# The output products of the last batch are begun inside the last attention units

## The chip, the cores and the metric

The kernel runs on one core of one Trainium2 chip, as a single launch. Times are device microseconds (us) of that core. The core's engines are named as in the profile: PE (TensorE, with PEld for its weight loads), DVE (VectorE), ACT (ScalarE), POOL (GpSimd) and SP (SyncE, which here only issues DMAs). "Line 913" or "L913" is a line of the kernel's file as the profile numbers it.

## The reference, cut to what matters

One block of a transformer with adaptive layer norm: attention, and then a mixture of eight experts in which every expert picks its 512 best rows. `x` is 8 batches of 1024 rows of 256; there are 16 heads of 64.

```python
mod = (_silu(c) @ wmod).reshape(8, 6, 1, -1)
sa, ca, ga, sb, cb, gb = (mod[:, i] for i in range(6))
# ga and gb are then kept at least 0.25 away from zero
h = _layernorm(x) * (1 + ca) + sa
x = x + ga * attention(h, w_qkv, w_o)
h = _layernorm(x) * (1 + cb) + sb
x = x + gb * experts(h, router_w, router_b, w1, b1, w2, b2)

def attention(inputs, w_qkv, w_o):
    q, k, v = three products of inputs with w_qkv, per head
    attn = softmax(einsum('bhqn,bhkn->bhqk', q, k) / 8)
    out = einsum('bhqk,bhkn->bhqn', attn, v)
    return concat_of_heads(out) @ w_o

def experts(x, ...):
    scores = softmax(x @ router_w + router_b)
    G, idx = top_k(scores.T, 512)      # over all 8192 rows
    y = scatter_add(relu(x[idx] @ w1 + b1) @ w2 + b2, times G)
```

The experts choose among all rows, so their search cannot begin before the router's scores of the last rows are known.

## The kernel before, in words

Attention is cut into 128 *units*. A unit is one batch, one pair of heads and one half (512) of the query rows; `unit(u)` gives them, two units to a pair, 16 to a batch. The last batch is number 7, and its pairs 4 to 7 are the last eight units; units 124 and 125 are pair 6, units 126 and 127 are pair 7. A unit has eight chunks of 128 keys. Per chunk, PE makes the scores (L397), ACT copies them out of PSUM (L406), DVE keeps the maximum (L414); when the maximum over all keys is turned and spread (L424 to L461), DVE subtracts it (L464), ACT takes the exponential (L467), PE multiplies with the values (L477), and POOL adds the exponentials of the chunks up for the denominator (L497, L500).

The order of all instructions is written by hand under a manual schedule: a loop over *steps*, four to a unit, so unit `u` begins at step `4u`. Its values are made six steps later (`LAG`). Everything that is not the core of a unit is put in by `at(step, place, function, ...)`; a step runs its places in a fixed order: "load" (DMA issues), "turn", the turned maximum, "head", scores, subtractions and maxima, "m1" (PE work ahead of the values), "post" (small DVE and ACT work), exponentials, values, sums on POOL, "pool", "m2". Each engine runs its own list in that order. G below stands for step 512, that of unit 127's turned maximum; the loop ends six steps later.

Denominators: `den_out` multiplies POOL's sum with ones (L516), ACT copies the result, and it goes to DRAM; `den_load` fetches it as 128 short rows, `den_inv` inverts it on DVE (L545) and stores it, `den_spread` reads it back spread over the partitions, `den_mul` scales the pair's rows on POOL (L562). Each of those DMAs is on SP's queue, in order. For pair 7 of batch 7, `last_load_den`, `last_inv` and `last_mul` do the same for each half, the second half on ACT's queue.

The output product `w_o` of a batch is made while the next batch's units run (`out_proj`, L618). The last batch has no next one. There the pairs 0 to 3 are loaded back in one DMA (`last_load`, step G-6, into the buffer of the large part of the projection weights, "wq1"), `last_gates` scales `wo` by the batch's gate on DVE (L738), and behind the loop a written list follows: for each tile of 128 rows, `add_pairs` makes eight pair products (L913), `add_x` adds the rows, takes mean and variance on DVE and the root of the variance on POOL (L106, L108) and starts the norm (L929), `norm` ends it (L937); then, for two tiles at a time, `turn` transposes them (L664), `route` makes the router's product (L676), and `score` takes the softmax (L691 to L707) and stores the rows. The sums of unit 127's chunks 0 to 3 come from POOL; chunks 4 to 7 of that unit are summed by PE (`pd_last`). After that the transposed scores (L1055) start the experts' search on DVE (L1068).

PSUM tiles come from pools: `ps_s` ("s") has two buffers, `ps_m` ("mm"), `ps_av` ("av") and `ps_b` ("less") one each; whoever takes a buffer waits until its former content has been read.

## Time and profile before

| what | us |
|---|---|
| median of 3 runs | 3381.17 |
| lowest and highest run | 3381.15, 3382.17 |
| the profiled execution | 3379.61 |
| its span, first to last instruction | 3377.9 |
| busy in the span: PE, DVE, ACT, POOL | 3312.0, 2718.1, 2468.7, 2716.6 |
| unit 127's maximum is turned | at 3013.39 |
| first output product of the last batch | at 3037.85 |
| the search starts on DVE | at 3076.09 |

Times with "at" count from the span's start. A line of the profile's timeline gives start, duration, engine, line, operation, what is written and read (with shapes) and how many instructions were merged; in brackets stands how long the engine was idle before it and what released it. In the groups of instructions, the columns behind the shape are the count, the busy time, the mean duration in ns, and the idle time before.

### The profile page before, as it was taken

Reading aid. Unit: us, or ns where it says so; the run is one execution under the profiler, and the core shown is the slowest. Engines: PE = TensorE matmul, PEld = TensorE weight load, DVE = VectorE, ACT = ScalarE, POOL = GpSimd, SP = SyncE. Lnnn points to the kernel's source line nnn. Section 1 sums busy time; section 2 is a strip of 40 time slices with the busy share of each in tenths; the row PEclk is TensorE's granted clock in tenths of the full one; section 3 lists DMA queues with packets and bytes.
Section 4 is the critical chain, followed back from the end, with each engine's and each line's share of the span. In section 5 each row is a group of like instructions: output and inputs, shape, how many; then the busy total and the mean of one; then the engine's idle time right before and its main releaser. Section 6 shows DMA issues by size and latency. Waiting matters only on the chain. (4 is left out here: it accounts for less than half of the span.)

```text
span 3377.9 us, 60194 instructions
## 1 busy us (share of the span) xinstructions
PE 3312.0 (98%) x23699; PEld 1343.1 (40%) x23699; DVE 2718.1 (80%) x3391; ACT 2468.7 (73%) x3079; POOL 2716.6 (80%) x1630
## 2 busy tenths in 40 slices
PE   9999999999999999999999999999999999986998
PEld 3333333333333333333333333333333333334666
DVE  6898888888888888888888888888888888886332
ACT  5888887778787877878787777878777787760221
POOL 4898888989898888989898888988898888891333
PEclk9999999999999999999999999999999999997999
DMA  4010012111121112111221112111221112124442
GB/s 83 17 46 28 26 48 56 42 47 53 45 63 42 47 53 56 44 47 51 47 61 42 47 53 56 48 42 52 48 59 42 47 53 58 51 77 145 108 100 45
DMA packets 184112, 183.68 MB, mean 54 GB/s; under 512 B 49148, under 2 KB 161292, under 8 KB 183700
## 3 DMA queue, kind: packets, MB, share of 16 engines
q1 hardware_dynamic: 167860, 158.44, 17.0%
q0 software_dynamic: 7168, 12.72, 1.9%
q10 hardware_dynamic: 8800, 8.68, 0.8%
q8 instruction: 186, 3.05, 0.4%
q14 instruction: 98, 0.80, 0.1%
HBM read 126.01 MB, written 62.16 MB: 56 GB/s over the span
## 5 line engine op out<-in xcount | busy, mean ns | idle before, releaser
L500 POOL TENSOR_TENSOR acc<-acc,p 128x1024 f32<-128x1024 f32 x764 | 1816.4, 2378 | 85.2 <-ACT p L467 37.4
L406 ACT COPY p<-s 128x1024 f32<-128x1024 f32 x1024 | 990.6, 1016 | 317.0 <-PE s L397 294.2
L464 DVE TENSOR_TENSOR p<-p,less 128x1024 f32<-128x1024 f32 x1024 | 1210.5, 1213 | 7.8 <-PE less L461 3.2
L414 DVE TENSOR_TENSOR top<-top,s 128x1024 f32<-128x1024 f32 x768 | 933.5, 1215 | 119.4 <-ACT p L406 104.5
L467 ACT ACTIVATE p<-p 128x1024 f32<-128x1024 f32 x1024 | 1025.3, 1052 | 3.4 <-DVE p L464 2.3
L397 PE MATMUL s<-qk,qk 64*128 64x512 f32 (+1 forms) x6144 | 996.6, 601 | 4.1 <-DVE top L414 4.1
L477 PE MATMUL av<-p,v 128*64 128x512 f32 x4096 | 995.1, 596 | 2.0 <-ACT p L467 2.0
L356 PE MATMUL pq<-hT,wq 128*64 128x512 f32 x2048 | 497.7, 607 | 0.7 <-ACT hT L308 0.7
L397 PEld LDWEIGHTS s<-qk,qk 64*128 64x128 f32 (+1 forms) x6144 | 314.8, 151 | 418.6 <-issue 218.5
L477 PEld LDWEIGHTS av<-p,v 128*64 128x64 f32 x4096 | 270.5, 137 | 487.1 <-issue 379.7
L497 POOL TENSOR_TENSOR acc<-p,p 128x1024 f32<-128x1024 f32 x128 | 304.8, 2381 | 15.9 <-ACT p L467 15.9
L432 DVE TENSOR_REDUCE tt<-tt 128x8 f32<-128x1024 f32 x128 | 157.7, 1232 | 178.6 <-PE tt L424 178.6
L356 PEld LDWEIGHTS pq<-hT,wq 128*64 128x64 f32 x2048 | 125.0, 136 | 350.3 <-issue 199.1
L377 PE MATMUL pv<-wq,hT 128*64 128x256 f32 x2048 | 249.2, 385 | 0.0
L634 POOL TENSOR_TENSOR ox<-ox,at 128x256 f32<-128x256 f32 x56 | 40.6, 726 | 243.2 <-DVE at L629 243.2
L618 PE MATMUL po<-wo,ot 128*64 128x256 f32 x1792 | 202.9, 379 | 0.0
L377 PEld LDWEIGHTS pv<-wq,hT 128*64 128x64 f32 x2048 | 135.7, 136 | 155.8 <-issue 57.1
L414 DVE TENSOR_TENSOR top<-p,s 128x1024 f32<-128x1024 f32 x128 | 154.8, 1209 | 46.9 <-ACT p L406 44.1
L618 PEld LDWEIGHTS po<-wo,ot 128*64 128x64 f32 x1792 | 128.7, 137 | 88.6 <-issue 24.3
L562 POOL TENSOR_TENSOR oT<-oT,rb 128x1024 f32<-128x1024 f32 x63 | 150.1, 2382 | 0.0
L1308 POOL DMA_INDIRECT out_dram<-eo,tok x32 | 53.6, 1675 | 115.8 <-DMA out_dram<-eo,tok 63.7
L361 ACT ACTIVATE qk<-pq 128x512 f32<-128x512 f32 x128 | 76.6, 598 | 95.7 <-PE pq L356 95.7
(198 smaller groups left out, 2254.2 us busy)
## 6 DMA issues: line engine op xcount, KB each, us to landing
rb<-rden_d SPq DMA_DIRECT2D x126, 256.0 KB
oT_d<-oT SPq DMA_DIRECT2D x60, 512.0 KB
ot<-oT_d SPq DMA_DIRECT2D x56, 512.0 KB
rows_d<-gb_d SPq DMA_DIRECT2D x8, 1024.0 KB
w<-in_L_ffn_w_dram SPq DMA_DIRECT2D x8, 1024.0 KB
w<-in_L_ffn_w_dram ACTq DMA_DIRECT2D x8, 1024.0 KB
rows_d<-row SPq DMA_DIRECT2D x62, 132.0 KB
lnx<-in_L_attn_inputs_dram SPq DMA_DIRECT2D x28, 256.0 KB
```

The source lines that it names most:

```text
L356: nc.tensor.matmul(pq[m * N : (m + 1) * N, :], wq_of(k, a, 2 * p + m), hTs[b][:, k, sl], start=(k == 0), stop=(k == KC - 1),)
L377: nc.tensor.matmul(pv[m * N : (m + 1) * N, i, :], hTs[b][:, k, t0 : t0 + N], wq_of(k, 2, 4 * g, 4), start=(k == 0), stop=(k == KC - 1),)
L397: nc.tensor.matmul(ps[k : k + n, j, :], kt[r, c * P + k : c * P + k + n], qt[r, h * QB : (h + 1) * QB], start=True, stop=True,)
L406: nc.scalar.copy(probs[u, c], ps)
L414: nc.vector.tensor_tensor(tops[u], probs[u, 0] if c == 1 else tops[u], ps, ALU.max)
L432: nc.vector.tensor_reduce(nm[:, 0, :], tt.rearrange("p r q k -> p q r k"), AX.XY, ALU.max, negate=True)
L464: nc.vector.tensor_tensor(probs[u, c], probs[u, c], less[u], ALU.add)
L467: nc.scalar.activation(probs[u, c], probs[u, c], AF.Exp)
L477: nc.tensor.matmul(avs[u][j * N : (j + 1) * N, :], v[:, c, hh * N : (hh + 1) * N], pT[:, j, :], start=(c == 0), stop=(c == NT - 1),)
L497: nc.gpsimd.tensor_tensor(sums[u], pts[0], pts[1], ALU.add)
L500: nc.gpsimd.tensor_tensor(sums[u], sums[u], pt, ALU.add)
L618: nc.tensor.matmul(po[m * N : (m + 1) * N, :], ot[:, p, m * N : (m + 1) * N], wo[:, p, :], start=(p == 0), stop=(p == NP - 1),)
```

## The change

It touches the last batch only.

- `part_out` makes the products of pairs 0 to 3 for the row tiles 4 to 7 at steps G-5, G-3, G-2 and G-1, and ACT copies each into a buffer; `part_add` adds all four to the rows of `x` on POOL. They need gated weights and the reloaded pairs early: `tail_set` (step G-56) takes the "wq0" buffer, loads the gate and builds a picking matrix, `tail_gate` multiplies four pairs of `wo` on POOL, and `tail_load` (formerly `last_load`) moves from step G-6 to G-9. `tail_gates` scales the other four pairs on DVE at step G.
- `fill` makes the pair products of tiles 0 and 1 between the units' work from step G to G+4, and all others behind the loop. Eight tiles share two PSUM tiles of `ps_s`.
- Pair 6 is handled in halves (`half_load`, `half_inv`, `half_spread`, `half_mul`), and the denominator of unit 125 moves from step G to G-1.
- Pair 7: `late_den` sums the chunks 4 to 7 on PE for unit 126 too; `late_inv` inverts the 128x256 denominators where they lie in PSUM, `late_spread` spreads them with two products by the picking matrix, `late_mul` scales. Nothing of it goes through DRAM.
- In `add_x` the first of the two variance steps is on DVE; the written list is reordered, and the norm of a tile (`add_norm`) stands behind the next tile's addition.

```diff
-            pool, tag = (ps_s, "s") if u == NSU - 1 else (ps_av, "av")
-            avs[u] = pool.tile([P, QB], F32, tag=tag, name=f"av{u}")
+            avs[u] = ps_av.tile([P, QB], F32, tag="av", name=f"av{u}")
...
+    def half_load(h):
+        d = tail["dq", h] = small.tile([P, 2 * QB // P], F32, tag="dq", name=f"dq_half{h}", bufs=2)
+        nc.sync.dma_start(
+            d, den_d[B - 1, NP - 2, h].rearrange("j s -> (j s)").rearrange("(p c) -> p c", p=P)
+        )
+
+    def half_inv(h):
+        nc.vector.reciprocal(tail["dq", h], tail["dq", h])
...
+    def half_mul(h):
+        at_hand[B - 1, NP - 2] = oTs[B - 1, NP - 2]
+        half = oTs[B - 1, NP - 2][:, h * QB : (h + 1) * QB]
+        nc.gpsimd.tensor_tensor(half, half, tail["rb", h], ALU.mult)
...
+        nc.sync.dma_start(tail["gate"], mod_d[B - 1 : B, :D].to_broadcast([P, D]))
+        nc.gpsimd.memset(tail["pick"], 0.0)
+        for j in range(2):
+            for i in range(2):
+                r = (2 * j + i) * 32
+                nc.gpsimd.memset(tail["pick"][r : r + 1, i, j * N : (j + 1) * N], 1.0)
+
+    def tail_gate(p):
+        nc.gpsimd.tensor_mul(tail["wo"][:, p, :], wo[:, p, :], tail["gate"])
+
+    def tail_gates():
+        w = wo[:, 4:, :]
+        nc.vector.tensor_tensor(
+            w, w, tail["gate"].unsqueeze(1).to_broadcast([P, NP - 4, D]), ALU.mult
+        )
...
+    def part_out(t):
+
+        if "part" not in tail:
+            tail["part"] = work.tile([P, 4, D], F32, tag="ot", name="part")
+        po = ps_m.tile([P, D], F32, tag="mm", name=f"part{t}")
+        add_pairs(po, t, 0, 4, 0, 3)
+        nc.scalar.copy(tail["part"][:, t - 4, :], po)
+
+    def part_add():
+        x1 = tail["x"][:, 4:, :]
+        nc.gpsimd.tensor_add(x1, x1, tail["part"])
...
+    def fill(t, p0, p1):
+        if not pos:
+            for i in range(2):
+                po = ps_s.tile([P, 2, QB], F32, tag="s", name=f"po_last{i}")
+                for k in range(4):
+                    pos[k // 2 * 4 + 2 * i + k % 2] = po[:, k % 2, k // 2 * D : (k // 2 + 1) * D]
+        add_pairs(pos[t], t, p0, p1, 0 if t < 4 else 4, NP - 1)
...
+    def late_inv(u):
+        tail["den"] = small.tile([P, QH], F32, tag="den", name=f"den{u}", bufs=2)
+        nc.vector.reciprocal(tail["den"], tail["pd"])
+
+    def late_spread(u):
+        rb = tail["rb"] = ps_m.tile([P, QB], F32, tag="mm", name=f"rb{u}")
+        for i in range(2):
+            nc.tensor.matmul(
+                rb[:, i * QH : (i + 1) * QH], tail["pick"][:, i, :], tail["den"],
+                start=True, stop=True,
+            )
...
-    for u in range(NSU - 1):
-        at(4 * u + 13 - max(0, u - NSU + 4), "m2", den_out, u)
+    for u in range(NSU - 2):
+        at(4 * u + (13 if u < NSU - 3 else 11), "m2", den_out, u)
...
-    at(4 * NSU - 2, "load", last_mods)
-    at(4 * NSU - 6, "load", last_load)
-    at(4 * NSU + 4, "load", last_load_den, 0)
-    at(4 * NSU + 4, "pool", last_gates)
-    at(4 * NSU + 5, "post", last_inv, 0)
+    G = 4 * NSU
+    at(G - 56, "load", tail_set)
+    for p in range(4):
+        at(G - 51 + 4 * p, "pool", tail_gate, p)
+    at(G - 9, "load", tail_load)
+    at(G - 2, "load", last_mods)
+    for t, g in zip((4, 5, 6, 7), (-5, -3, -2, -1)):
+        at(G + g, "m1", part_out, t)
+    for h, g in ((0, -2), (1, 0)):
+        at(G + g, "load", half_load, h)
+        at(G + g + 1, "post", half_inv, h)
+        at(G + g + 2, "load", half_spread, h)
+        at(G + g + 3, "pool", half_mul, h)
+    at(G, "post", tail_gates)
+    at(G, "m1", fill, 0, 0, 4)
+    at(G + 1, "m1", fill, 0, 4, 6)
+    at(G + 1, "m2", late_den, NSU - 2, range(4, NT))
+    at(G + 2, "post", late_inv, NSU - 2)
+    at(G + 2, "m1", fill, 0, 6, 7)
+    at(G + 2, "m1", fill, 1, 0, 4)
+    at(G + 3, "m1", late_spread, NSU - 2)
+    at(G + 3, "post", late_mul, NSU - 2)
+    at(G + 3, "m1", fill, 1, 4, 7)
+    for t in range(2):
+        at(G + 4, "m1", fill, t, 7, 8)
+        at(G + 4, "pool", add_x, t)
+    at(G + 4, "pool", part_add)
+    at(G + 5, "m1", late_den, NSU - 1, range(4, 6), False)
+    at(G + 5, "pool", add_norm, 0)
...
-                if u1 < NSU - 1 or gm1 < 2:
+                if u1 < NSU - 2 or gm1 < 2:
...
+        late_den(NSU - 1, range(6, NT), True, False)
...
-            (add_x, 0), (add_pairs, 3, 0, NP), (add_x, 1), (norm, 0), (add_x, 2), (norm, 1),
-            (last_mul, 1), (norm, 2), (add_x, 3), (add_pairs, 4, 0, NP), (norm, 3), (turn, 0),
-            (add_x, 4), (norm, 4), (add_pairs, 5, 0, NP), (add_x, 5), (route, 0), (norm, 5),
-            (turn, 2), (add_pairs, 6, 0, NP), (score, 0), (add_x, 6), (route, 2), (norm, 6),
-            (turn, 4), (add_pairs, 7, 0, NP), (score, 2), (add_x, 7), (route, 4), (norm, 7),
-            (score, 4), (turn, 6), (route, 6), (score, 6),
+            (late_inv, u), (fill, 2, 0, NP), (add_norm, 1), (late_spread, u), (late_mul, u),
+            (fill, 3, 0, NP), (add_x, 2), (turn, 0), (fill, 4, 4, NP), (add_x, 3), (add_norm, 2),
+            (route, 0), (fill, 5, 4, NP), (add_x, 4), (add_norm, 3), (turn, 2), (fill, 6, 4, NP),
+            (score, 0), (add_x, 5), (add_norm, 4), (route, 2), (fill, 7, 4, NP), (add_x, 6),
+            (add_norm, 5), (score, 2), (turn, 4), (add_x, 7), (add_norm, 6), (route, 4),
+            (add_norm, 7), (score, 4), (turn, 6), (route, 6), (score, 6),
```

## The prediction

> **What bounds the kernel now.** The page shows 98% busy for PE and 80% for DVE and POOL, but that is a mean over 3,378 us, and the change touches the last 90 us of attention only. So I read first the windows by stage (columns: stretch, its length, then busy us and instruction count of PE, PEld, DVE, ACT, POOL, the granted clock, DMA share, GB/s).

> ```profile
> 2987.00:3013.00 26.00, 21.77 (x152) 6.47 (x148) 24.34 (x30) 20.77 (x24) 22.93 (x18) 1.00 0.35 116
> 3013.00:3038.00 25.00, 17.70 (x148) 5.53 (x150) 17.12 (x22) 12.77 (x19) 24.45 (x11) 1.00 0.09 24
> 3038.00:3069.00 31.00, 31.00 (x316) 20.98 (x314) 16.24 (x49) 3.10 (x8) 10.14 (x22) 1.00 0.22 69
> 3069.00:3076.00 7.00, 2.70 (x30) 1.59 (x28) 3.75 (x16) 1.57 (x5) 5.20 (x23) 0.85 0.59 196
> ```

> The last two units have PE free for 4.2 and 7.3 us; then PE alone is the bound for 31 us; then a chain of small steps leads to the search. Next the timeline of PE in the third and fourth stretch (start, duration, what, idle before):

> ```profile
> 3037.28 0.64 PE L516 MATMUL pd_last<-acc,ones 128*32 128x256 f32 x8 [1.82 <-POOL acc L500]
> 3037.85 1.95 PE L913 MATMUL po_last<-wo,oT_last 128*64 128x256 f32 x16
> ...
> 3060.46 1.95 PE L913 MATMUL po_last<-wo,oT_last 128*64 128x256 f32 x16
> 3062.24 1.90 PE L913 MATMUL po_last<-wo,oT 128*64 128x256 f32 x16
> 3063.96 0.59 PE L676 MATMUL pl<-rw,h2T 128*64 128x8 f32 x16
> ...
> 3071.66 0.44 PE L664 MATMUL pth<-ident,rows_last 128*128 128x128 f32 x2 [2.13 <-DVE rows_last L937]
> ```

> The output products of all eight row tiles start only at 3037.85, when POOL's sum of unit 127 is in. One tile (eight pairs) takes 3063.96 - 3060.46 = 3.50, a pair 0.44. Then DVE's timeline, for the price of a tile and for the end of the stage:

> ```profile
> 3051.51 0.41 DVE L921 TENSOR_TENSOR x_last<-x_last,po_last 128x256 f32<-128x256 f32 x1
> 3051.96 0.43 DVE L116 BATCH_NORM_STATS2 st_b<-x_last 128x6 f32<-128x256 f32 x1
> 3052.42 0.18 DVE L117 BATCH_NORM_AGGREGATE mv_b<-st_b 128x2 f32<-128x6 f32 x1
> 3052.64 0.48 DVE L929 SCALAR_TENSOR_TENSOR row<-x_last,mv_b,mod 128x256 f32<-128x256 f32 x1
> 3053.04 0.48 DVE L937 SCALAR_TENSOR_TENSOR row<-row,rs_b,mod 128x256 f32<-128x256 f32 x1
> ...
> 3071.12 0.48 DVE L937 SCALAR_TENSOR_TENSOR rows_last<-rows_last,rs_b,mod 128x256 f32<-128x256 f32 x1 [0.43 <-POOL rs_b L108]
> ...
> 3076.09 0.75 DVE L1068 TENSOR_SCALAR half<-p_sc 128x256 int32<-128x256 int32 x2 [0.84 <-PE p_sc L1055]
> ```

> From start to start: the four steps before the norm take 0.45 + 0.46 + 0.22 + 0.40 = 1.53, the norm 0.40. The norm of tile 7 starts at N = 3071.12; the search starts 4.97 later. All behind that is moved as a whole, so the question is what N becomes. Last the groups by shape, for the reciprocals and the scaling of the weights:

> ```profile
> L545 DVE RECIPROCAL dq<-dq 128x16 f32<-128x16 f32 x63 | 14.6, 231 | 0.0
> L699 DVE RECIPROCAL rd<-rd 128x2 f32<-128x2 f32 x32 | 5.3, 166 | 1.1
> L738 DVE TENSOR_TENSOR wo<-wo,mod 128x1024 f32<-128x1024 f32 x2 | 5.0, 2534 | 0.0
> L629 DVE TENSOR_TENSOR at<-po,mod 128x256 f32<-128x256 f32 x56 | 23.7, 424 | 56.3 <-PE po L618 56.3
> ```

> **The change part by part.** Times are those of the profiled execution: 3379.61, of which the span is 3377.9; the median shown is 3381.17, 1.56 above it. G is the step of unit 127's transposed maximum, 3013.39 before.

> *Tiles 4 to 7, pairs 0 to 3, at steps G-5, G-3, G-2, G-1.* Four groups of 4 pairs, 1.75 each, 7.0 of PE. From 2987.42 (scores of step G-5) PE's list up to the maximum of unit 127 is: ten score chunks 9.35, ten value chunks 9.0, the four groups 7.0, two denominators 1.14, transposes 0.72 + 0.45, row spread 0.65: 28.3, so the maximum is turned at 3015.7 instead of 3013.39. PE had 4.2 idle there, so 7.0 costs 2.3. DVE, some 0.75 late after the first group, is ready at 3014.1 and no longer the bound. Four ACT copies of 0.38 lie beside DVE.

> *Denominator of unit 125 from step G to G-1.* 0.57 on PE (in the sum above). At 3019.59 the routing product sat 1.42 behind that denominator's copy; this goes.

> *Pair 6 in halves.* SP: store, load, store, two spreads per half. Half 0's load stands behind the load of `mod7`, issued 3009.14 when POOL finished the last row of batch 6; its inverse (0.2) comes on DVE after the last maximum at 3014, 2 us after landing. Half 1: copied 3015.8, loaded by about 3020 to 3022 (the rows for such a load, 3038.39 to 3043.60, give 5.2), inverted on DVE at 24.9 between two subtractions, 2.7 to 4.8 spare. It would hold DVE's subtractions, so exponentials, values and all behind, if late. Cost: 0.4 of DVE.

> *Loads moved.* `tail_load` (2048 + 1024 KB) goes from 2981.46 to about 2960, when the last weights are read (PE 2957.99 + 1.94). In the windows that transfer filled 2983 to 2992, about 9 us. Behind it in SP's queue now are an output store (2966.39), `ox` and `ot` (2967.58), which PE wants at 2983.87; at worst they are done near 2976. Cost nothing, 8 us of cover. `tail_set` at G-56 and its five fills and four products on POOL, 0.73 each, some 4 us in all: POOL stood idle 4.22, 0.64 and 2.17 before three late L634, which takes them up.

> *Weights scaled once, at step G:* 2.53 on DVE, in a hole of 4.00 behind the split maximum (DVE waited for the routing product until 3020.28). Ready at 3021.1; subtractions start at 3021.5, before 3020.59. Before it was 4.99 at 3030, also hidden.

> *Unit 126's chunks 4 to 7 summed by PE instead of POOL:* 4 x 0.45 = 1.8 more on PE, 9.7 less on POOL, whose last sum then ends by 3032 and ends the wait of 1.82 at 3037.28.

> *Last denominators on chip.* Twice a reciprocal 128x256. No row has that; 128x2 takes 166 ns and 128x16 231, so 4.6 ns an element and 1.35 for 256. Ends: 0.42 (L629, as many elements, one pass) and 1.75 (from the dearest 128x16 row, 253 ns); I take 1.35, the slope of most rows. [...] Two picking products of 128x256 each time: 0.22 per record, two records each, 0.88; ends 0.44 and 1.75. In exchange two round trips through DRAM go, the second 3038.39 to 3053.44; PE never waited for it, so that alone is worth nothing.

> *PE from the maximum at 3015.7 to the last denominator:* turn 0.7, 16 pair products 7.0, 12 value chunks 10.8, row turns and spread 0.5, routing 0.57, ten denominator groups 4.5, picks 0.88: 25.0. The pick waits for the reciprocal: subtractions from 3021.5, six at 1.145 plus 0.2, plus 1.35 gives 3029.95, where PE arrives at 3029.7: 0.3 more. End 3041.0, against 3037.85 before, but with 32 of 64 pair products done.

> *From there.* PE: tile 2 3.5, pick 0.88, tile 3 3.5: 3048.9 (call it E). By the order of the built program the addition of tile 2 waits for tile 3's product, that of 4 for 5's, and 6 for 7's, since tiles share a PSUM tile. A tile on DVE now is 1.53 plus 0.20 for the variance step moved from POOL (ends 0.16 and 0.25), 1.72. DVE after E: two tiles 3.44, norm 0.40, router 0.40; waits for tile 5's product until E+4.77; tile 4 and norm 3 to E+6.89; now the score of tiles 0, 1 wants an exponential that ACT has queued behind the copy of tiles 2, 3's transposes, which wait for norm 3: transposes 0.48, copy 0.68, exponential 0.5, and DVE stands until E+8.5; scores 0.62, tile 5 1.72, norm and router 0.80, tile 6 1.72, norm and scores 1.02, tile 7 1.72, norm 0.40, router 0.40: N = E+16.95 = 3065.85. PE needs only E+11.4 for all its products: DVE is the bound. Gain 5.25.

> *What is late next.* POOL fills its constants after the score copies of tiles 4, 5, which now stand ahead of them: the last constant is in at N+6.5 where the search wants it at N+6.1: 0.45 lost. Weights and rows land far ahead of the first expert product (3127.79).

> Sum: -5.25 + 0.45 = -4.8: 3374.8 on the profiled execution's scale, **3376.4** on the median's.

> Unknown: reciprocals -0.4 to +0.4, picks -0.9 to +1.7, variance step 0.3 either way, hops between engines 0.8, PE's clock when the experts start (first relus 0.85 apart, later half that, so about 1 either way). Together -7.0 to -2.3.

> **The rivals.**
> - *PE stays the bound to the end*: additions start with their own tile and the exponential does not hold DVE. Then tile 7's product ends at E+9.3, N = E+11.7 and the gain is 10.5 less 0.45: 3371.1. For it: before, DVE hardly made PE wait in this stretch. Against: DVE's list from E to N is 14.8 long without any hole, so it needs both; the hole alone gone gives N = E+15.2, a gain of 6.5, 3374.7.
> - *Nothing comes of it*: the four groups cost their whole 7.0 (score chunks arrive late and DVE's maxima too), 4.7 more than in the sum: 3381. For it: DVE was 94% busy there. Against: its maxima had the scores early.
> - *Slower: half 1's denominators land late and hold DVE's queue.* Its load is behind a spread that waits for POOL's product of pair 5 (3013.77) and a buffer. Beyond 2.7 to 4.8 late, every us is one us; 11.6 more makes it slower by 0.2%, 3388. For it: the similar load before held DVE for 8.46. Against: SP's queue is otherwise empty here.

> **How the numbers follow.** Two runs of this kernel can be told apart at about 0.2%, 6.8 us. My sum (-7 to -2.3, nearly all within 0.2%) 0.55; PE-bound end 0.23, most of it faster by over 0.2%; nothing 0.10; slower, by the queue, 0.12. With the sum's own edge: faster 0.25, same 0.63, slower 0.12. The likeliest case's own range is 3374.2 to 3379.0. For 8 in 10 I take 3371.5 (the PE-bound end) to 3380.5.

> **What would show it.** Unit 127's maximum turned near 3015.7, its last denominator on PE near 3041, no POOL wait before it; a DVE wait of about 2 us on ACT's exponential at the first score; N near 3065.9; reciprocal 128x256 about 1.35. Wrong if DVE waits for `dq_half1`, if PE has holds between 3016 and 3041, or if DVE's tiles take other than 1.7.

## The result, and the profile after

The changed kernel takes **3376.17 us** (median of 20 runs, 3375.05 to 3378.03), the kernel before 3381.16 beside it (20 runs, 3380.21 to 3383.82): a ratio of 0.9985, 95% interval 0.9978 to 0.9992. The interval lies below 1, so the kernel is faster, but by less than the 0.2% (6.8 us) from which the prediction counts a change; the time is 0.2 us from the forecast. A repeat of both, later, gave 3376.79 against 3379.82, 0.9990 (0.9981 to 0.9999), so the gain is 3 to 5 us, and the hit to 0.2 is partly luck.

The profiled execution after has 3377.24, its span 3375.4, against 3379.61 and 3377.9. Single executions differ by 1 us ahead of the part that was changed. So all places below are counted from **S**, the start of the scores of step G-5, the last thing on PE ahead of the first part group: 2987.42 before, 2988.35 after. First the windows by stage of the kernel after (columns as before):

```profile
2987.00:3013.00 26.00, 26.00 (x202) 10.66 (x200) 23.78 (x30) 19.54 (x24) 22.96 (x18) 1.00 0.18 52
3013.00:3038.00 25.00, 25.00 (x234) 12.07 (x234) 19.40 (x31) 14.78 (x20) 16.85 (x9) 1.00 0.10 29
3038.00:3069.00 31.00, 25.89 (x240) 14.83 (x230) 17.88 (x59) 3.71 (x10) 8.41 (x15) 0.93 0.17 57
3069.00:3076.00 7.00, 2.85 (x36) 1.96 (x36) 3.66 (x15) 1.08 (x3) 5.67 (x28) 0.50 0.63 194
```

PE, which had 4.2 and 7.3 us free in the first two stretches, has none now; in the third, which it filled before, it has 5.1 free. The granted clock in the third fell from 1.00 to 0.93. PE's timeline of the kernel after shows where:

```profile
3016.37 0.67 PE L424 MATMUL tt<-ident,top 64*128 64x64 f32 x16
...
3041.72 1.95 PE L630 MATMUL po_last<-tail_set,tail_rest 128*64 128x256 f32 x16
...
3049.99 0.66 PE L779 MATMUL pth<-ident,row 128*128 128x128 f32 x4
...
3056.90 0.44 PE L779 MATMUL pth<-ident,row 128*128 128x128 f32 x2 [1.81 <-DVE row L705]
3057.27 3.34 PE L630 MATMUL po_last<-wo,oT 128*64 128x256 f32 x16
3060.38 0.91 PE L791 MATMUL pl<-rw,h2T 128*64 128x8 f32 x16
3061.14 1.93 PE L630 MATMUL po_last<-wo,oT 128*64 128x256 f32 x16
```

The turned maximum comes at S+28.0, the first product behind the last denominator at S+53.4 (call it T0), the end of tile 3's product, E, at S+61.6. Then PE stands 1.81 for DVE's norm of tile 3, and tile 6's half product (its pairs 4 to 7) takes 3.1 from start to start instead of 1.75. On DVE's timeline of the kernel after, the additions (L687) and the end:

```profile
3050.11 0.42 DVE L687 TENSOR_TENSOR x_last<-x_last,po_last 128x256 f32<-128x256 f32 x1 [2.86 <-PE po_last L630]
...
3054.76 0.42 DVE L687 TENSOR_TENSOR x_last<-x_last,po_last 128x256 f32<-128x256 f32 x1 [0.70 <-PE po_last L630]
...
3058.43 0.17 DVE L813 TENSOR_REDUCE rd<-ex 128x2 f32<-128x16 f32 x1 [1.59 <-ACT ex L806]
...
3063.12 0.42 DVE L687 TENSOR_TENSOR x_last<-x_last,po_last 128x256 f32<-128x256 f32 x1 [1.40 <-PE po_last L630]
...
3067.88 0.48 DVE L705 SCALAR_TENSOR_TENSOR tail_set<-tail_set,rs_b,mod 128x256 f32<-128x256 f32 x1
...
3073.35 0.76 DVE L1131 TENSOR_SCALAR half<-p_sc 128x256 int32<-128x256 int32 x2 [0.84 <-PE p_sc L1118]
...
3074.94 0.17 DVE L1145 TENSOR_SCALAR cand<-upto 128x4 f32<-128x4 f32 x1 [0.33 <-POOL upto L1114]
```

Additions 2, 4 and 6 each wait for PE's next tile, and the first score waits 1.59 for an exponential. N, the norm of tile 7, is at S+79.53 (before S+83.70), the search at S+85.00 (before S+88.67): 3.7 earlier. From the search to the end the profile has 302.05 after and 301.8 before. Last the group of the new reciprocal:

```profile
L667 DVE RECIPROCAL den<-pd 128x256 f32<-128x256 f32 x2 | 3.5, 1754 | 2.4 <-PE pd L515 2.4
```

### The profile page after: what moved, and what is told of

It is laid out like the page before. It is cut to its first block, busy times and chain, and to the rows that moved or that the text cites. A ratio compares the mean times of both kernels' runs of the same rounds, so it can differ in the third digit from the quotient of the medians.

```text
span 3375.4 us, 60263 instructions
## 1 busy us (share of the span) xinstructions
PE 3317.2 (98%) x23739; PEld 1346.8 (40%) x23739; DVE 2718.8 (81%) x3399; ACT 2470.6 (73%) x3081; POOL 2711.8 (80%) x1629
```

## The experiments

The theory at the start: PE's free time in the last two units now holds 14 us of products, which is the gain, and from E on DVE bounds the end; the rivals were PE as the bound to the end, and early products that are worth nothing. In what follows, the part groups are the products of `part_out`, a pick is the pair of products by the picking matrix (L672), a turn is PE's transposing of two tiles (L779), and the hole is DVE's wait of 1.59 at the first score. Each run was timed against the kernel before on the same chip. All that was measured, with places from S:

| kernel | T0 | E | N | search | median | before beside it | ratio, 95% interval |
|---|---|---|---|---|---|---|---|
| before | 50.43 | | 83.70 | 88.67 | 3381.16 | | |
| after | 53.37 | 61.64 | 79.53 | 85.00 | 3376.17 | 3381.16 | 0.9985 (0.9978 to 0.9992) |
| after, repeated (r1) | 53.37 | 61.64 | 79.52 | 84.99 | 3376.79 | 3379.82 | 0.9990 (0.9981 to 0.9999) |
| no part groups (e1) | 51.38 | 59.65 | 82.77 | 88.26 | 3380.39 | 3380.47 | 1.0001 (0.9991 to 1.0010) |
| tiles 0, 1 late (e2) | 50.63 | 65.80 | 82.03 | 87.50 | 3379.90 | 3380.47 | 1.0000 (0.9991 to 1.0009) |
| the same, pick later (e2b) | 49.06 | 64.24 | 80.58 | 86.06 | 3378.16 | 3381.28 | 0.9991 (0.9982 to 1.0000) |
| neither early start (e7) | 47.05 | 62.23 | 85.36 | 90.83 | 3383.96 | 3380.83 | 1.0008 (0.9999 to 1.0017) |
| before + PE's sums (b1) | 49.65 | | 82.94 | 88.48 | 3380.74 | 3381.28 | 0.9998 (0.9989 to 1.0007) |
| denominators by DRAM (e6) | 53.39 | 60.44 | 79.39 | 85.15 | 3376.07 | 3379.82 | 0.9989 (0.9980 to 0.9998) |
| exponential early (e3) | 53.38 | 61.65 | 79.51 | 84.98 | 3376.04 | 3380.47 | 0.9987 (0.9978 to 0.9996) |
| PE kept busy (e4) | 53.38 | 61.65 | 77.87 | 83.35 | 3375.24 | 3380.47 | 0.9984 (0.9975 to 0.9993) |
| both of these (e34) | 53.37 | 61.64 | 77.85 | 83.32 | 3375.05 | 3380.65 | 0.9983 (0.9974 to 0.9992) |
| even and odd tiles (e5) | 53.38 | 61.65 | 76.12 | 81.60 | 3374.13 | 3381.28 | 0.9978 (0.9969 to 0.9987) |
| that and a new order (v2) | 53.38 | 61.65 | 73.96 | 78.93 | 3371.68 | 3381.28 | 0.9972 (0.9961 to 0.9982) |

The two profiled executions of the changed kernel, with PE's half clock at the same product in both, have the same places to 0.02 us (T0 53.37 and 53.37, N 79.53 and 79.52), so the places tell apart what the medians cannot; the medians follow the column of the search.

### The part groups taken out (e1)

```diff
-    for t, g in zip((4, 5, 6, 7), (-5, -3, -2, -1)):
-        at(G + g, "m1", part_out, t)
...
-    at(G + 4, "pool", part_add)
...
-            ... (fill, 4, 4, NP) ... (fill, 5, 4, NP) ... (fill, 6, 4, NP) ... (fill, 7, 4, NP)
+            ... (fill, 4, 0, NP) ... (fill, 5, 0, NP) ... (fill, 6, 0, NP) ... (fill, 7, 0, NP)
```

> The changed kernel without the four part groups: tiles 4 to 7 take all eight pairs behind the last denominator, as before the change; everything else stays. S is the start of the scores of step G-5 (2988.35 in the changed kernel); there the maximum of unit 127 is turned at S+28.0, tile 3's product ends at E = S+61.6 and the norm of tile 7 starts at N = S+79.5. Theory (DVE is the bound from E to N; the part groups take 7.0 us of PE, of which only 2.3 stand in the way of the maximum): the maximum is turned 2.0 to 2.3 earlier, E is 1.5 to 2.3 earlier, and tile 5's product, which DVE waits for, then ends 0.9 later, at E+8.0; tile 7's some 2.7 later, since the turn of tiles 2 and 3 waits for DVE's norm in between. N 2 to 3.5 later than in the changed kernel. Rival, PE is the bound to the end: N later by 7.0 - 2.3 = 4.7 with no DVE work left between a tile's product and its addition. Rival, the parts are worth nothing: N as before or up to 2 earlier.

Tiles 4 to 7 then begin their sums with pair 0 instead of pair 4. The maximum is turned 2.04 earlier (S+25.98), E 1.99 earlier, N 3.24 later, all as the theory had it, and with that the time is that of the kernel before. But the execution after had PE at half its clock for one product, and this one had not. Against the kernel with a full clock there (e4, below), N is 4.90 later, which is about the rival's figure, 4.7. DVE's waits on PE in the kernel without part groups show that PE's products are on the path to the end:

```profile
3055.61 0.42 DVE L687 TENSOR_TENSOR x_last<-x_last,po_last 128x256 f32<-128x256 f32 x1 [3.12 <-PE po_last L630]
...
3065.75 0.42 DVE L687 TENSOR_TENSOR x_last<-x_last,po_last 128x256 f32<-128x256 f32 x1 [3.12 <-PE po_last L630]
```

### Tiles 0 and 1 behind the last denominator (e2, e2b)

```diff
-    at(G, "m1", fill, 0, 0, 4)
-    at(G + 1, "m1", fill, 0, 4, 6)
...
-    at(G + 3, "m1", fill, 1, 4, 7)
...
-            (late_inv, u), (fill, 2, 0, NP), (add_norm, 1), ...
+            (late_inv, u), (fill, 0, 0, NP), (fill, 1, 0, NP), (add_x, 0), (add_x, 1), (part_add,),
+            (fill, 2, 0, NP), (add_norm, 0), (add_norm, 1), ...
```

> The changed kernel with the products, additions and norm of tiles 0 and 1 moved behind unit 127's last denominator; the part groups, the denominators and pair 6 stay as they are. 7.0 us of PE is taken out of the steps from the maximum to the last denominator. Theory (those steps are bound by DVE and ACT behind the last exponential, which starts at 3031.40 in the changed kernel, so that little of the 7.0 was free time at the end): the last denominator ends about 5.5 earlier than in the changed kernel (S+53.4, S as in the other kernels), the four products then take 14.0 plus the pick 1.1, E is 1.0 to 2.0 later, and N with it. Rival, the holes were all real: the last denominator ends only where it ends now, and N is 5 to 7 later. Rival, PE alone bounds this stretch: the denominator ends 7.0 earlier and N does not move.

A miss: with 7.0 of products taken out ahead of it, T0 came only 2.74 earlier, and E 4.16 later. PE's timeline of that kernel says why, at the pick of unit 126's denominators:

```profile
3029.29 1.13 PE L672 MATMUL rb<-den,tail_set 128*128 128x256 f32 x4 [2.52 <-DVE den L667]
3030.35 3.65 PE L476 MATMUL av<-p,v 128*64 128x512 f32 x16
```

The pick waits for DVE's reciprocal, and four chunks' value products stand behind it in PE's order. In the changed kernel early products cover that wait. The next run moves the pick behind the value products:

```diff
-    at(G + 3, "m1", late_spread, NSU - 2)
-    at(G + 3, "post", late_mul, NSU - 2)
+    at(G + 3, "m2", late_spread, NSU - 2)
+    at(G + 4, "post", late_mul, NSU - 2)
```

> The run with the products of tiles 0 and 1 behind the last denominator, with one thing more: the pick of unit 126's denominators (two products on PE that need DVE's reciprocal) is issued behind the value products of step G+3 and not ahead of them. In the run before it PE stood 2.52 at this pick with value products queued behind it, and the last denominator ended only 2.7 earlier than in the changed kernel, where 5.5 had been forecast. Theory (that queueing is what was missed): the wait goes, the last denominator ends 2.0 to 3.2 earlier than in the run before it (S+50.6), the product of tile 3 ends as much earlier (S+65.8 there), and N 1.5 to 3 earlier than S+82.0. Rival (the value products wait for the exponentials anyhow): the wait moves to ACT's exponentials and the end does not move by more than 0.7.

T0 comes 1.57 earlier, N 1.45: more than the rival allows, less than the theory says, as a wait of 0.81 for the same reciprocal stays. With the better of the two orders the early products of tiles 0 and 1 move T0 from S+49.06 to S+53.37: of their 7.0, 4.3 stand in the way and 2.7 are free. N of e2b against the full clock of e4: 2.71.

### Neither early start (e7)

Both edits together (e1 and e2b).

> The changed kernel without either early start: no part groups, and the products of tiles 0 and 1 behind the last denominator, with the pick of unit 126 behind the value products as in the better of the two runs on that. What is left of the change is pair 6 in halves, the last denominators on chip, PE's share of unit 126's sums, the moved loads, the weights scaled once and the new written list. Each undone alone, the part groups are worth 4.9 and the early tiles 2.7 at N, against the execution with a full clock (S+77.9). Theory (these two are where the gain is, and the rest costs: the picks 1.06 each on PE, waits for the next tile's product, the turns' wait of 1.81): by the sum of the two N is at S+85 to 86; by the layout, last denominator at S+47 to 47.5, then 28.0 of products, 1.1 for the pick, 5.3 for turns and routers as before and one or two waits of 1.8, S+83.5 to 85.5. Either way no earlier than before (S+83.7). Rival (the rest gains too, since the sums of unit 126 no longer hold PE, and PE is the bound to the end): S+81 to 82.5.

N at S+85.36, where the sum of the two, 77.87 + 4.90 + 2.71, gives 85.48; the search 2.2 later than before the change. So the early products are worth 7.5 at N against the full clock (5.8 against the changed kernel as it ran, S+79.53), and what is left of the change costs 1.7 there and 0.5 more up to the search. It ends the denominators 3.4 earlier than before (T0 at 47.05 against 50.43), and loses 5.0 from there to N: the second pick, 1.06, and twice the wait of 1.81 at a turn, which the list before did not have in this place, make 4.7 of it.

```profile
3061.01 0.44 PE L779 MATMUL pth<-ident,row 128*128 128x128 f32 x2 [1.81 <-DVE row L705]
...
3071.15 0.44 PE L779 MATMUL pth<-ident,row 128*128 128x128 f32 x2 [1.81 <-DVE row L705]
```

### PE's share of unit 126's sums, alone (b1)

In the kernel before:

```diff
-                if u1 < NSU - 1 or gm1 < 2:
+                if u1 < NSU - 2 or gm1 < 2:
                     add_up(u1, gm1)
...
         pd = ps_m.tile([P, QH], F32, tag="mm", name=f"pd{u}")
-        den_mm(pd, sums.pop(u))
+        cs = range(4, NT) if u == NSU - 2 else ()
+        for c in cs:
+            den_mm(pd, probs.pop((u, c)), start=(c == 4), stop=False)
+        den_mm(pd, sums.pop(u), start=not cs)
```

> The kernel before, with one part of the change alone: the probabilities of unit 126's chunks 4 to 7 are summed by PE (16 small products more, 1.8 us) and no longer by POOL (four additions, 9.7 us less). In the kernel before PE waits 1.82 for POOL's last sum at 3037.28, and half a us at 3028.36 for the one ahead of it. Theory (POOL's sums set the end of the last unit there, and PE has the room for 1.8 more): the wait of 1.82 goes, the output products begin 1.0 to 1.8 earlier than S+50.4, where S is the start of the scores of step G-5 (2987.42 before); N, S+83.7 before, moves with them, since PE is the bound from there on. Rival (PE's 1.8 stand in the way of the value products and of the last exponential's): no gain, or up to 0.8 later.

The wait of 1.82 is gone, but the products begin only 0.78 earlier and N 0.76: short of the theory's 1.0; the search is only 0.19 earlier. PE's list now has the 1.8 itself, so the sums of unit 126 end later, and with them ACT's copy of the denominators (S+42.95, before S+41.69). The last two exponentials stand behind that copy in ACT's queue and are late by the same 1.26; PE's wait of 0.70 for them was there before too. In this execution PE also ran at half its clock from 3021.81 to 3025.23, but its value products ended at S+40.5 as before. PE's timeline of that kernel:

```profile
3033.88 2.02 PE L477 MATMUL av<-p,v 128*64 128x512 f32 x8 [0.70 <-ACT p L467]
3035.84 1.93 PE L519 MATMUL pd_last<-p,ones 128*32 128x256 f32 x32
3037.59 0.61 PE L519 MATMUL pd_last<-acc,ones 128*32 128x256 f32 x8
```

### Unit 127's denominators through DRAM (e6)

```diff
-            (late_inv, u), (fill, 2, 0, NP), (add_norm, 1), (late_spread, u), (late_mul, u),
-            (fill, 3, 0, NP), (add_x, 2), (turn, 0), (fill, 4, 4, NP), (add_x, 3), (add_norm, 2),
-            (route, 0), (fill, 5, 4, NP), ...
+            (far_load, u), (fill, 2, 0, NP), (add_norm, 1), (far_inv, u),
+            (fill, 3, 0, NP), (add_x, 2), (turn, 0), (add_x, 3), (add_norm, 2), (route, 0),
+            (far_mul, u), (fill, 4, 4, NP), (fill, 5, 4, NP), ...
```

> The changed kernel with unit 127's denominators going through DRAM again (copied by ACT, stored, loaded as 128x8, inverted, stored, spread by two loads, the product of pair 7 then on POOL, which is idle there) in place of the reciprocal 128x256 and the pick on PE; the written list is only reordered so far that the addition of tile 3 and the router of tiles 0 and 1 stand ahead of tile 4's product. Before the change this trip took 3038.39 to 3053.44, 15.0 us, and PE did not wait for it. Theory (with part of tiles 4 to 7 done ahead, PE comes to pair 7 of tile 4 at S+62 to S+63, and the trip, begun at S+54, ends at S+69, the product of pair 7 at S+70.5): PE waits some 7 there, and N is 2 to 4 later than S+79.5. Rival (the trip stays hidden, and on-chip inversion buys nothing, as before): N within 0.5, or 1 earlier, since the pick of 1.06 on PE goes.

The three `far` functions store, invert and spread the denominators through DRAM as the `half` ones do for pair 6, and POOL multiplies. The rival is right: N 0.14 earlier, the median the same as the repeat of the changed kernel on that chip (3376.07 and 3376.79). PE waited 1.71 for POOL's product of pair 7, not 7. The 15.0 that I had read as the trip's length were no such thing: in the kernel before, DVE's multiplication at 3053.44 came late because of its place in DVE's list; the last loads had been issued at 3045.32. Here POOL multiplies at 3051.87, 9.2 behind the issue of the store at 3042.70. PE's timeline of this kernel:

```profile
3053.18 2.38 PE L630 MATMUL po_last<-wo,oT 128*64 128x256 f32 x20 [1.71 <-POOL oT L1029]
```

Its clock stayed full, so against e4 the on-chip inversion of unit 127 is worth 1.5 at N, the difference in the list included; against the changed kernel as it ran, nothing.

### The hole at the first score, and PE's clock (e3, e4, e34, r1)

The first edit moves one exponential in ACT's queue, the second puts three products on PE that nothing reads:

```diff
-            ... (add_x, 4), (add_norm, 3), (turn, 2), ...
+            ... (add_x, 4), (add_norm, 3), (early_exp, 0), (turn, 2), ...
```

> The changed kernel with the exponential of tiles 0 and 1 put into ACT's queue ahead of the copy of tiles 2 and 3's transposes; DVE's order is the same. The wait of 1.59 at DVE's first score (ex7_0) goes in every case. Theory from the trace of the changed kernel (DVE waits 0.34 and 1.40 right behind it for PE's products of tiles 6 and 7, so the hole is followed by another): these two waits grow by what the first one lost, and N moves by 0 to 0.4. Rival, as the prediction had it (DVE without this hole is the bound): N 1.25 to 1.6 earlier.

```diff
+        def warm(n):
+            po = ps_b.tile([P, D], F32, tag="less", name=f"warm{n}")
+            for k in range(3):
+                nc.tensor.matmul(po, ident, wo[:, k, :], start=(k == 0), stop=(k == 2))
...
-            ... (add_x, 4), (add_norm, 3), (turn, 2), ...
+            ... (add_x, 4), (add_norm, 3), (warm, 0), (turn, 2), ...
```

> The changed kernel with three throw-away products of 128x256 on PE ahead of the turn of tiles 2 and 3, where PE stood idle for 1.81 us at 3055.09 to 3056.90; nothing reads them, and all that the reference computes is still computed. Theory (that idle time is why the granted clock was 0.56 in the stretch that followed, and tile 6's product took 3.1 us instead of 1.75): tile 6's product takes 1.75 to 1.9 again, DVE's wait for tile 7's product becomes under 0.3, and N is 1.2 to 1.7 earlier than S+79.5. Rival (the clock falls there for another reason, such as a clock that looks at a longer time, or DVE's and POOL's load): the products still take 3.1, the throw-away ones delay the turn by up to 0.3, N is 0 to 0.4 later.

The hole is worth nothing: N moves by 0.02, as the wait right behind it grows from 0.34 to 2.00; the 1.40 after that stays. DVE's timeline with the early exponential:

```profile
3060.82 0.17 DVE L796 TENSOR_TENSOR lg<-pl,rb 128x16 f32<-128x16 f32 x1 [2.00 <-PE pl L791]
...
3062.59 0.42 DVE L687 TENSOR_TENSOR x_last<-x_last,po_last 128x256 f32<-128x256 f32 x1 [1.40 <-PE po_last L630]
```

The throw-away products are worth 1.66 at N. PE's timeline with them:

```profile
3055.69 1.56 PE L1024 MATMUL warm<-wo,ident 128*128 128x256 f32 x6
3057.09 0.38 PE L779 MATMUL pth<-ident,row 128*128 128x128 f32 x2
3057.94 0.44 PE L779 MATMUL pth<-ident,row 128*128 128x128 f32 x2 [0.47 <-DVE row L705]
3058.30 1.95 PE L630 MATMUL po_last<-wo,oT 128*64 128x256 f32 x16
```

Since the run with the exponential had the half clock too, both edits together:

> The changed kernel with both small edits of the earlier runs: the exponential of tiles 0 and 1 ahead of the copy of the next transposes, and the three throw-away products ahead of the turn of tiles 2 and 3. The run with the exponential alone had PE at half the clock behind the turn, so it did not tell what the hole of 1.59 is worth at the full clock; with the products alone N was at S+77.9 and DVE's wait for tile 7's product 0.16. Theory (the hole is followed at once by the wait for PE's products of tiles 6 and 7, clock or no clock): these waits grow by 1.5, N at S+77.6 to S+77.9. Rival (with the clock full DVE is the bound, and the hole is its own time, as the prediction had it): N 1.25 to 1.6 earlier, S+76.3 to S+76.6.

N at S+77.85, 0.02 from the products alone: at the full clock too, the hole hides nothing but the wait for PE. So DVE is not the bound by itself.

For the clock, windows of 3.4 us of the kernel after (the granted clock is the column ahead of the last two); it changed at 3057.67 and 3061.08, and the other limits lie one length away:

```profile
3054.26:3057.67 3.41, 1.60 (x14) 0.74 (x11) 1.97 (x6) 0.24 (x1) 0.72 (x1) 1.00 0.11 38
3057.67:3061.08 3.41, 3.41 (x30) 2.17 (x28) 2.40 (x9) 0.73 (x3) 1.04 (x3) 0.50 0.26 83
3061.08:3064.50 3.42, 2.36 (x24) 1.30 (x22) 1.62 (x7) 0.49 (x2) 0.00 (x0) 1.00 0.14 46
```

> The changed kernel once more, unchanged, for a second profiled execution of it on the chip of the run above. PE's idle time of 1.81 ahead of tile 3's transposes should be there again. If the granted clock of tile 6's product depends only on the program, it is 0.5 to 0.6 again, N is S+79.5 within 0.2. If it depends on where the idle time falls in the clock's stretches of 3.41 us, which the program does not set, it may be 1.00 here, tile 6's product then takes 1.75 and N is S+77.9 within 0.2.

The repeat had the half clock at the same place, S+69.7 against S+69.3, tile 6's product took 2.77 from start to start, and N was at S+79.52. The two repeat each other, but that does not show that the program sets the clock. In the trace of the kernel after, the stretches from one change of the clock to the next, from 3057.67 on, are 3.41, 6.83, 47.79, 3.41, 10.24 and 238.93 long, that is 1, 2, 14, 1, 3 and 70 times 3.413; in the kernel before, from 3073.94 on, 44.37, 3.41, 10.24 and 238.93, or 13, 1, 3 and 70 times. So I take windows of that length. Every trace here has a later fall of the clock, and counted back from it in steps of 3.413 us the limits of the windows lie at another distance from S in each execution: S+69.3, S+69.7 and, in e3, S+68.7. In e5 one is at S+67.1, which would cut the changed kernel's idle time (S+66.7 to S+68.6) in two. In the two executions of the changed kernel and in e3 the whole idle time of 1.81 lies inside one window, which leaves PE busy for 1.60 or 1.61 of it, and the next window is at half clock. In e2, e2b, e6 and e7, which have the same idle time at the same turn, a limit falls inside it, PE is busy for at least 1.66 in each window, and the clock stays full. The windows of e7, counted back from its fall at 3074.20, where the idle time is 3059.20 to 3061.01:

```profile
3057.14:3060.55 3.41, 2.06 (x18) 1.06 (x14) 1.57 (x6) 0.00 (x0) 0.24 (x1) 1.00 0.10 36
3060.55:3063.96 3.41, 2.95 (x26) 1.98 (x28) 1.68 (x8) 0.97 (x3) 0.74 (x3) 1.00 0.01 2
```

In e1 the idle time begins 0.05 behind a limit, PE is busy for 1.60, and the clock stays full: that edge is open. So I estimate from these profiles that the 1.66 is a cost that an execution of the changed kernel may have or not have, by where the windows fall; both of its profiled executions had it, and the timed runs without a trace do not tell how many had it.

### Even and odd tiles apart, and a new order (e5, v2)

```diff
-                    pos[k // 2 * 4 + 2 * i + k % 2] = po[:, k % 2, k // 2 * D : (k // 2 + 1) * D]
+                    pos[2 * k + i] = po[:, k % 2, k // 2 * D : (k // 2 + 1) * D]
```

> The changed kernel with only the places of the eight tiles in PSUM exchanged: the even tiles share one PSUM tile and the odd ones the other, so that the addition of tile 2, 4 or 6 waits for its own product and not for that of the next one. Work and orders are the same. In the changed kernel these waits of DVE are 2.86, 0.70 and 1.40, N is S+79.5. Theory (the end is a chain in which DVE waits for PE's next tile, and PE's turn waits for DVE's norm, 1.81; no engine is full): the addition of tile 2 starts right behind the multiplication of pair 7, at S+58.9 instead of S+61.8; tile 4's 0.7 earlier; the wait of the turn of tiles 2 and 3 falls from 1.81 to about 0.5; N is 2.5 to 4 earlier, S+75.5 to S+77. Rival (DVE's work from E to N, 14.8, is the bound, as the prediction had it): what is won at tile 2 is DVE's own time, so N can be no more than 1.6 earlier, one tile's work. Rival (the wait is only moved to another place): N within 0.4.

One index. Addition 2 starts at S+58.83 instead of S+61.76, the wait at the turn is 0.32, the clock stays full, N is 3.41 earlier, the time 3374.13. Of that, 1.66 is what the clock alone gives in e4, so the waits themselves are worth 1.75, little over the 1.6 that the rival allowed for DVE's own time; the run speaks for the theory, but not by itself.

```profile
3047.33 0.41 DVE L687 TENSOR_TENSOR x_last<-x_last,po_last 128x256 f32<-128x256 f32 x1
...
3053.44 0.41 DVE L687 TENSOR_TENSOR x_last<-x_last,po_last 128x256 f32<-128x256 f32 x1
```

The second run keeps this and writes the list anew:

```diff
+            (late_inv, u), (fill, 2, 0, NP), (add_norm, 1), (late_spread, u), (late_mul, u),
+            (fill, 3, 0, NP), (add_x, 2), (turn, 0), (add_x, 3), (add_norm, 2), (fill, 4, 4, NP),
+            (route, 0), (early_exp, 0), (add_norm, 3), (add_x, 4), (fill, 5, 4, NP), (turn, 2),
+            (add_x, 5), (add_norm, 4), (score, 0), (fill, 6, 4, NP), (route, 2), (early_exp, 2),
+            (add_norm, 5), (add_x, 6), (fill, 7, 4, NP), (turn, 4), (add_x, 7), (add_norm, 6),
+            (route, 4), (early_exp, 4), (add_norm, 7), (score, 2), (score, 4), (turn, 6),
+            (route, 6), (score, 6)
```

> The changed kernel with the places in PSUM of the run with even and odd tiles, and the written list at the end in another order: each addition is issued ahead of the next tile's product, norm 3 ahead of addition 4, the exponentials of tiles 0, 2 and 4 ahead of the next copy of transposes, the scores of tiles 2 to 5 behind the last norm. The same work. Worked out from the rows of the changed kernel (tile 1.59 on DVE, product of half a tile 1.75, norm 0.40, router 0.35, copy 0.6): turn of tiles 2 and 3 at 3054.6 without a wait, addition of tile 6 at 3058.0, of tile 7 at 3059.6, N at 3062.0, that is S+73.7 against S+79.5: 5 to 6 earlier, and the search 4.5 to 5.5 earlier, as POOL's constants then come some 0.6 late instead of 0.33. Rival (DVE or the clock takes it back): 2 to 3.5 earlier, no better than the even and odd tiles alone.

N at S+73.96 (worked out: 73.7), the search 6.07 earlier than in the changed kernel and 9.74 earlier than before; POOL's constants are no longer waited for. **3371.68 us**, 0.9972 of the kernel before (0.9961 to 0.9982), beats both kernels. PE's turn of tiles 2 and 3 now runs in one piece; PE's line and DVE's end:

```profile
3054.02 0.66 PE L779 MATMUL pth<-ident,row 128*128 128x128 f32 x4
...
3061.67 0.48 DVE L705 SCALAR_TENSOR_TENSOR tail_set<-tail_set,rs_b,mod 128x256 f32<-128x256 f32 x1
```

From E to N this kernel takes 12.3, against 17.9 in the changed kernel and 16.2 with the full clock. DVE waits 0.12 and once 0.81 in it, and no more: in that order DVE is the bound.

## Why the prediction was right, point by point

The time fell inside the range of the likeliest case, and the turned maximum, the denominators and E came where that case had them; what it named as the bound behind E was wrong, as told behind the list. By its steps, in places from S (the forecast's places less 2987.42):

- **The turned maximum**, forecast S+28.3: S+28.0. Four groups cost 2.0 on the path of their 7.0 (forecast 2.3; e1).
- **The last denominator**, forecast S+53.6: S+53.4; **E**, forecast S+61.5: S+61.6. In that sum a pick is 1.06 from start to start instead of 0.88, and PE's wait at the first pick is nil.
- **The reciprocal 128x256**, taken as 1.35: 1.75, the upper end. The slope from 2 to 16 elements per partition does not carry to 256: 1754/256 is 6.9 ns an element, not 4.6. Nothing hung on the size in the changed kernel: DVE had 2.37 free ahead of the second.
- **Weights scaled once**: 1.52, forecast 2.53; the subtractions began at S+33.3, forecast S+34.1.
- **Half 1's denominators**, the rival for slower: `dq_half1` is inverted without a wait. **The loads moved**: PE has no idle time where they might have been late.
- **A tile on DVE**: 1.60 from start to start, forecast 1.72, since the variance step takes 0.07 and not 0.20.
- **Waits of additions 2, 4 and 6 for the next tile**: there. Addition 4 is at E+4.77, as forecast to the digit.
- **The hole at the first score**, forecast 1.6: 1.59.
- **N**, forecast E+16.95: E+17.89. Two terms: six tiles cheaper by 0.12 (-0.7), and **PE's clock, halved for one stretch of 3.41 us, +1.66** (e4). The sum had the clock only as an unknown at the experts, not in this stretch.
- **From N to the search**, taken over as 4.97: 5.47, with PE at half the clock from 3067.9 on, so from the start of this stretch; before, it fell only 2.8 behind N.
- **POOL's constants**, forecast 0.45 late: 0.33.

The sum was -4.8; in the profiles the search starts 3.7 earlier and waits 0.33, -3.3, as the clock's 1.66 and the 0.5 up to the search were not in it and 0.7 was too much. These misses partly cancel, and the medians, which moved by 5.0 and in the repeat by 3.0, lie to both sides of the profiles: that is the luck in the hit.

What failed is a step of the rivals and the name of the bound. "The hole alone gone gives N = E+15.2": it gives nothing, at half and at full clock (e3, e34). The forecast had the reason in its own numbers: PE has all its products only at E+11.4, and DVE with its hole reaches addition 6 at E+11.6. With the hole gone DVE comes to the same place earlier and waits there. So "DVE is the bound" was wrong for this order: the end is a loop through both engines, from tile 3's product over two additions, a wait for tile 5 and the norm of tile 3 to the turn on PE, and from there over tiles 6 and 7 on PE back to DVE. The rival "PE stays the bound to the end" (E+11.7, 3371.1) did not come, for the reason given against it; it needs both the own-tile additions and the early exponential, and with these and a new order v2 gets E+12.3 and 3371.7.

That a round trip through DRAM less "is worth nothing" holds as measured (e6). That POOL's wait of 1.82 goes is right, but alone it is worth 0.8 at N and 0.2 at the search (b1).

## What to carry to other kernels

Work that is moved into an engine's free time is worth what it leaves behind at the end less what it delays on the way: here 14 us of products moved were worth 7.5 at the full clock, of which the rest of the change took 1.7 back. Before a hole is taken out, look at the next wait of the same engine, and put the bounds of all engines at that place beside each other. Look which results share a PSUM tile: here the reader of the first waited for the product of the second (2.86, 0.70 and 1.40), and one index decided over 3.4 us, 1.66 of them by the clock.

## What the runs showed of the hardware that was not expected

```profile
3048.60 3.09 DVE L705 SCALAR_TENSOR_TENSOR row<-row,rs_b,mod 128x256 f32<-128x256 f32 x2
```

```profile
3045.84 1.01 DVE L705 SCALAR_TENSOR_TENSOR row<-row,rs_b,mod 128x256 f32<-128x256 f32 x2
```
